# A four-layer graph network on one core: another order of the PE work of layers 2 and 3

## The chip, the cores and the metric

One core of one Trainium2 chip. The metric is the device time of one execution in microseconds (us). The kernel before took 2206.6 us (median of 4 runs, 2201.6 to 2208.3, so within 0.3%). Engines are named as in the profile: PE (matrix multiply), PEld (its weight loads), DVE, ACT, POOL, SP.

## The reference, cut to what matters

`x` is 128 graphs x 64 nodes x 256 features in fp32. Four residual layers follow each other; the change touches only the last two, which are attention inside one graph:

```python
h = relu(layernorm(x)); x = x + L2(h)     # layer 2: one head, + adj, causal mask, softmax, @ Wo
h = relu(layernorm(x)); x = x + L3(h)     # layer 3: four heads, mask adj == 0, softmax
```

Layers 0 and 1 (graph convolutions and LSTM windows) end at about 1752 us of 2206.

## The kernel before: the parts that matter

The kernel works through 16 chunks of 512 rows. Layers 2 and 3 of a chunk are four generators, each cut into units by `yield`. A table says in which order PE does the units; **only PE's order is fixed by hand**. DVE, ACT and POOL get their order from the scheduler, which works with the dependences and its own idea of durations.

```python
def rsqrt(dst, src, eps):                                     # for every layer norm, on POOL
    nc.gpsimd.tensor_scalar(dst, src, eps, None, op0=OP.add)                      # L80
    nc.gpsimd.tensor_tensor(dst, dst, mhalf[:, : dst.shape[1]], OP.pow)           # L81
...
def layernorm_relu(dst, src, name):     # names: st, mv (DVE), rstd (POOL), nmr (DVE), h (ACT)
    ...                                 # suffix _e: the norm of layer 2, _f: of layer 3
def softmax(s, n, name):                # n = 16 for layer 3, 4 for layer 2
    nc.vector.tensor_reduce(mx, s, AX.X, OP.max)                                  # L507
    nc.gpsimd.tensor_tensor(s, s, mx[...], OP.subtract)                           # L508
    nc.scalar.activation(s, s, AF.Exp)                                            # L509
    nc.vector.tensor_reduce(sm, s, AX.X, OP.add)                                  # L511
    nc.vector.reciprocal(rs, sm)                                                  # L513
    nc.vector.tensor_mul(s, s, rs[:, :, None].to_broadcast([P, n, T]))            # L514
...
# A = layer2_scores: [layer norm, transposes tc_e] [q, L558 is the copy of half of it] [v] [scores L567, softmax]
# B = layer2_out:    [transposes of the softmax] [output, added to x]
# C = layer3_scores: [layer norm, transposes tc_f] [q, k] [scores L616, softmax] [v]
# D = layer3_out:    [transposes L523, copies att: L528 on ACT, L530 on DVE] [output L643, store]
ROUND = (("A", 0), ("A", 0), ("A", 0), ("D", -2), ("C", -1), ("D", -2), ("C", -1), ("B", 0),
         ("A", 1), ("B", 0), ("C", -1), ("C", -1))
...
with tc.manual_schedule(engines={mybir.EngineType.PE}):
    unit("A", 0)
    for c in range(NCH + 2):
        for stage, d in ROUND:
            unit(stage, c + d)
```

`("C", -1)` in round c is the next unit of layer 3's scores for chunk c - 1.

Of the kernel before, what the change touches and what calls it, by code (L numbers as in the profile page):

```python
# [19 lines left out]
def kernel(  # L20
# [23 lines left out]
    B, T, D = x.shape  # L44
# [11 lines left out]
    NCH = B * T // CH  # L56
# [403 lines left out]
    with tc.tile_pool(name="w2", bufs=1) as w2p, tc.tile_pool(name="l2", bufs=2) as l2:  # L460
# [169 lines left out]
        def layer3_out(c):  # L630
# [14 lines left out]
            for r in range(2):  # L645
# [4 lines left out]



        stages = {"A": layer2_scores, "B": layer2_out, "C": layer3_scores, "D": layer3_out}
        ROUND = (("A", 0), ("A", 0), ("A", 0), ("D", -2), ("C", -1), ("D", -2), ("C", -1), ("B", 0),
                 ("A", 1), ("B", 0), ("C", -1), ("C", -1))
        units = {}

        def unit(stage, c):
            if 0 <= c < NCH:
                if (stage, c) not in units:  # L660
                    units[stage, c] = stages[stage](c)
                next(units[stage, c])

        with tc.manual_schedule(engines={mybir.EngineType.PE}):
            unit("A", 0)
            for c in range(NCH + 2):
                for stage, d in ROUND:
                    unit(stage, c + d)


# [44 lines left out]
```

## Time and profile before

| | before |
|---|---|
| median of 4 runs | 2206.6 us |
| span of the profiled run | 2205.7 us |
| PE busy | 2101.8 us (95%) |
| layers 2 and 3: one steady round | 26.20 us |
| wait of layer 2's scores for q (L567 for L558) | 1.09 to 1.15 us in each of 13 rounds |
| waits of the last two softmax transposes (L523) | 6.64 and 4.92 us |

A wait in square brackets in a timeline is the idle time of that engine just before the row and what ended it.

### The profile page before, as it was taken

How to read it: one execution, taken by the hardware profiler on the slowest of the kernel's cores; microseconds unless marked ns; L12 is line 12 of the kernel's file. 1: busy time of each engine (PE TensorE's matmuls, PEld its weight loads, DVE VectorE, ACT ScalarE, POOL GpSimd, SP SyncE). 2: the span in 40 equal slices, each digit the busy share in tenths (PEclk: the TensorE clock that was granted, in tenths of full speed). 3: DMA queues.
4: the chain of work that ended last, by engine and by line, in shares of the span. 5: the costliest groups of instructions: out<-in, count | busy, mean ns of one | idle time of the engine just before them, and what ended most of it. 6: DMA issues, size and time to landing. Idle time of an engine off the chain costs nothing.

```text
span 2205.7 us, 24595 instructions
## 1 busy us (share of the span) xinstructions
PE 2101.8 (95%) x10117; PEld 1339.7 (61%) x10117; DVE 852.5 (39%) x1848; ACT 792.1 (36%) x1433; POOL 168.8 (8%) x216
## 2 busy tenths in 40 slices
PE   6999959999999999999999999999999899999996
PEld 3553435576577468468567657656746756666664
DVE  5643433223323322332332322323222256666664
ACT  3544413233333233333333422333333344444442
POOL 2100010001000000000100100000000011112211
PEclk9999969999999999999999999999999999999998
DMA  3100050000000000000000000000000100000000
GB/s 97 58 20 0 0 186 10 10 1 10 2 9 1 10 10 1 10 10 1 10 10 1 10 10 1 0 0 1 1 0 1 34 11 21 20 21 21 21 20 29
DMA packets 30127, 37.88 MB, mean 17 GB/s; under 512 B 1856, under 2 KB 27456, under 8 KB 30016
## 3 DMA queue, kind: packets, MB, share of 16 engines
q1 hardware_dynamic: 27600, 27.89, 4.1%
q0 software_dynamic: 2256, 8.40, 1.0%
q8 instruction: 79, 1.29, 0.2%
q14 instruction: 32, 0.26, 0.0%
q10 hardware_dynamic: 160, 0.03, 0.0%
HBM read 27.93 MB, written 8.39 MB: 16 GB/s over the span
## 4 chain that ended last, share of the span: by engine, by line
PE 77%; issue 10%; DVE 7%; POOL 3%; DMA 2%; ACT 1%; SPq 0%; POOLq 0%; DVEq 0%; ACTq 0%
PE g L369 32%; PE g L376 17%; PE z L250 5%; PE z L234 3%; PE p_q L500 3%; PE u L340 3%; PE p_k L500 2%; PE v L328 2%; DMA xt<-in_x_dram 2%; PE agg_b L161 1%; PE agg_c L161 1%; PE tr L523 1%; DVE s L514 1%; PE o L643 1%; PE o L588 1%
## 5 line engine op out<-in xcount | busy, mean ns | idle before, releaser
L369 PE MATMUL g<-hT,wih 128*128 128x256 f32 (+2 forms) x2496 | 826.7, 483 | 3.6 <-DVE hT L400 2.7
L369 PEld LDWEIGHTS g<-hT,wih 128*128 128x128 f32 x2496 | 465.0, 188 | 313.1 <-issue 182.4
L382 ACT ACTIVATE gate<-g,bias 128x256 f32<-128x256 f32 (+2 forms) x624 | 350.4, 562 | 820.0 <-PE g L376 648.1
L376 PE MATMUL g<-hs,whh 128*128 128x256 f32 (+2 forms) x1536 | 435.8, 437 | 0.0
L376 PEld LDWEIGHTS g<-hs,whh 128*128 128x128 f32 x1536 | 291.3, 190 | 132.2 <-issue 62.0
L386 DVE TENSOR_TENSOR cell<-cell,gate 128x256 f32<-128x256 f32 (+2 forms) x96 | 48.7, 507 | 449.7 <-ACT gate L382 449.7
L391 DVE TENSOR_TENSOR cell<-gate,gate 128x512 f32<-128x512 f32 (+2 forms) x80 | 48.2, 602 | 213.1 <-ACT gate L382 213.1
L234 PE MATMUL z<-agg,w_sb 128*128 128x512 f32 x256 | 117.5, 613 | 8.6 <-DVE agg L227 7.2
L250 PE MATMUL z<-h,w_sb 128*128 128x512 f32 x256 | 112.1, 601 | 5.0 <-ACT h L245 5.0
L392 ACT ACTIVATE gate<-cell 128x256 f32<-128x256 f32 (+2 forms) x176 | 89.8, 510 | 50.7 <-DVE cell L391 40.3
L410 POOL COPY hn<-hT 128x512 f32<-128x512 f32 x32 | 35.9, 1197 | 784.8 <-DVE hT L400 784.8
L400 DVE TENSOR_TENSOR hT<-gate,gate 128x512 f32<-128x512 f32 (+2 forms) x80 | 48.0, 600 | 114.0 <-PE g L369 96.9
L250 PEld LDWEIGHTS z<-h,w_sb 128*128 128x128 f32 x256 | 49.4, 193 | 67.7 <-issue 57.5
L234 PEld LDWEIGHTS z<-agg,w_sb 128*128 128x128 f32 x256 | 48.6, 195 | 67.4 <-issue 49.0
L395 DVE TENSOR_TENSOR hs<-gate,gate 128x256 f32<-128x256 f32 (+2 forms) x96 | 47.7, 497 | 69.8 <-ACT gate L392 49.6
L385 DVE TENSOR_TENSOR gate<-gate,gate 128x256 f32<-128x256 f32 (+2 forms) x96 | 47.7, 497 | 55.8 <-ACT gate L382 55.8
L508 POOL TENSOR_TENSOR s<-s,mx 128x256 f32<-128x256 f32 (+1 forms) x32 | 40.3, 1259 | 340.3 <-DVE mx L507 251.8
L495 ACT COPY v<-v 128x512 f32<-128x512 f32 x64 | 37.0, 578 | 76.6 <-PE v L492 76.6
L500 PE MATMUL p_q<-hT,w_sb 128*128 128x512 f32 x128 | 61.9, 606 | 0.3 <-DVE hT L175 0.3
L500 PE MATMUL p_k<-hT,w_sb 128*128 128x512 f32 x128 | 60.1, 592 | 0.0
L492 PE MATMUL v<-w_sb,hT 128*128 128x256 f32 x256 | 59.5, 386 | 0.0
L151 ACT ACTIVATE h<-xs,nmr_b,rstd_b 128x256 f32<-128x256 f32 x64 | 34.5, 590 | 69.6 <-DVE nmr_b L149 69.6
(153 smaller groups left out, 2068.1 us busy)
## 6 DMA issues: line engine op xcount, KB each, us to landing
xt<-in_x_dram SPq DMA_DIRECT2D x32, 512.0 KB, 3.8
out_dram<-o SPq DMA_DIRECT2D x16, 512.0 KB, 2.9
wih<-in_wih_t_dram POOLq DMA_DIRECT2D x4, 1024.0 KB, 13.4
whh<-in_whh_t_dram POOLq DMA_DIRECT2D x3, 1024.0 KB, 18.2
w_sb<-in_w_dram SPq DMA_DIRECT2D x1, 768.0 KB, 4.2
wqkv_sb<-in_wqkv_dram SPq DMA_DIRECT2D x1, 768.0 KB, 4.5
w_sb<-in_w1t_dram POOLq DMA_DIRECT2D x1, 512.0 KB, 4.9
w_sb<-in_w2t_dram POOLq DMA_DIRECT2D x1, 512.0 KB, 5.8
```

What stands on the lines that cost most here:

```text
L234: nc.tensor.matmul(ps, w1_sb[:, k, m * P : (m + 1) * P], agg[:, k, :], start=(k == 0), stop=(k == KD - 1))
L250: nc.tensor.matmul(ps, w2_sb[:, k, m * P : (m + 1) * P], h1[:, k, :], start=(k == 0), stop=(k == KH - 1))
L340: nc.tensor.matmul(ps[:, i, :], v[:, k, j * P : (j + 1) * P], wg1_sb[:, k, :], start=(k == 0), stop=(k == KD - 1))
L369: nc.tensor.matmul(banks[q][:, :n].rearrange("p (j w e) -> p j w e", w=nw, e=2), wi[:, k, o], hv[:, k, :, cols, :], start=(k == 0), stop=( ...
L376: nc.tensor.matmul(banks[q][:, :n], wh[:, k, o], hs[:, k, :n], start=False, stop=(k == KD - 1))
L382: nc.scalar.activation(g[q], banks[q][:, :n], AF.Tanh if q == 2 else AF.Sigmoid, bias=bs[:, q * KD + c : q * KD + c + 1])
L386: nc.vector.tensor_mul(cell[c], cell[c], g[1])
L391: nc.vector.tensor_mul(cell[c], g[0], g[2])
L392: nc.scalar.activation(g[2], cell[c], AF.Tanh)
L400: nc.vector.tensor_mul(hv[:, c, :, cols, :], o.rearrange("p (j w e) -> p j w e", w=nw, e=2), t.rearrange("p (j w e) -> p j w e", w=nw, e=2))
L492: nc.tensor.matmul(ps[:, i, :], hT[:, k, j * P : (j + 1) * P], w[:, k, first : first + D], start=(k == 0), stop=(k == KD - 1))
L500: nc.tensor.matmul(ps, w[:, k, m * P : (m + 1) * P], hT[:, k, :], start=(k == 0), stop=(k == KD - 1))
```

## The change

Intent: q of layer 2 goes ahead of layer 3's v, so that its copies are done before the scores want them; and in the last rounds chunk 15's layer 2 and the work of its neighbours are mixed so that the last softmaxes have matmuls beside them.

```diff
-        ROUND = (("A", 0), ("A", 0), ("A", 0), ("D", -2), ("C", -1), ("D", -2), ("C", -1), ("B", 0),
-                 ("A", 1), ("B", 0), ("C", -1), ("C", -1))
+        ROUND = "A0 C-2 A0 A0 D-2 C-1 D-2 C-1 B0 A1 B0 C-1"
+        LAST = "A0 A0 A0 C-2 C-1 D-2 B0 D-2 B0 C-1 C-1 C-1 C0 C0 D-1 C0 D-1 C0 D0 D0"
...                                     # run(order, c) does the units of such a string
-            unit("A", 0)
-            for c in range(NCH + 2):
-                for stage, d in ROUND:
-                    unit(stage, c + d)
+            run("A0", 0)
+            for c in range(NCH - 1):
+                run(ROUND, c)
+            run(LAST, NCH - 1)
```

More of the change, by code (lines that the diff above doesn't have):

```diff
@@ L653, with run @@
         stages = {"A": layer2_scores, "B": layer2_out, "C": layer3_scores, "D": layer3_out}
-        ROUND = (("A", 0), ("A", 0), ("A", 0), ("D", -2), ("C", -1), ("D", -2), ("C", -1), ("B", 0),
-                 ("A", 1), ("B", 0), ("C", -1), ("C", -1))
+        ROUND = "A0 C-2 A0 A0 D-2 C-1 D-2 C-1 B0 A1 B0 C-1"
+        LAST = "A0 A0 A0 C-2 C-1 D-2 B0 D-2 B0 C-1 C-1 C-1 C0 C0 D-1 C0 D-1 C0 D0 D0"
         units = {}
-        def unit(stage, c):
-            if 0 <= c < NCH:
-                if (stage, c) not in units:
-                    units[stage, c] = stages[stage](c)
-                next(units[stage, c])
+        def run(order, c):
+            for step in order.split():
+                stage, at = step[0], c + int(step[1:])
+                if 0 <= at < NCH:
+                    if (stage, at) not in units:
+                        units[stage, at] = stages[stage](at)
+                    next(units[stage, at])
         with tc.manual_schedule(engines={mybir.EngineType.PE}):
-            unit("A", 0)
-            for c in range(NCH + 2):
-                for stage, d in ROUND:
-                    unit(stage, c + d)
+            run("A0", 0)
+            for c in range(NCH - 1):
+                run(ROUND, c)
+            run(LAST, NCH - 1)
 def kernel(**inputs):
```

## The prediction

> **What bounds the kernel now.** I read the page's busy shares, then the waits of the PE in the stretch that the change touches, then the timeline of one round engine by engine, then the timeline of the end. Times are us from the span's start.
>
> ```profile
> PE 2101.8 (95%) x10117; PEld 1339.7 (61%) x10117; DVE 852.5 (39%) x1848; ACT 792.1 (36%) x1433; POOL 168.8 (8%) x216
> ```
>
> PE is the bound: nothing else is above 39%. The change keeps every matmul and only reorders them, so it can win no more than PE idle time inside layers 2 and 3 (1755 to 2206), plus matmuls that ran at a low clock after such idle time. The PE's waits from 1720 on, columns total us, times, longest:
>
> ```profile
> PE tr L523 <- DVE s L514: 15.0, 3, 6.6
> PE s L567 <- DVE q L558: 14.8, 13, 1.2
> ```
>
> These 30 us (1.4% of the span) are nearly all there is. The second line is one wait in each of 13 rounds: layer 2's scores wait for the copy of the second half of q. The first is 3.5 us at the very start (not touched) and 6.6 and 4.9 us in the last two rounds. One steady round on PE, then on DVE, POOL and ACT (start, duration, line, work):
>
> ```profile
> 2063.83 3.60 PE L500 MATMUL p_q<-hT,wqk_sb 128*128 128x512 f32 x8
> 2072.29 1.15 PE L567 MATMUL s<-hT,q 128*64 128x64 f32 x30 [1.15 <-DVE q L558]
> 2073.37 1.09 PE L523 MATMUL tr<-ident,s 128*128 128x128 f32 x8
> 2074.30 1.04 PE L173 MATMUL tc_f<-ident,h 128*128 128x128 f32 x8
> 2075.27 1.16 PE L643 MATMUL o<-v,att 64*64 64x64 f32 x64
> ...
> 2067.65 0.16 DVE L149 SCALAR_TENSOR_TENSOR nmr_f<-mv_f,rstd_f 128x4 f32<-128x4 f32 x1 [1.96 <-POOL rstd_f L81]
> 2070.05 0.16 DVE L149 SCALAR_TENSOR_TENSOR nmr_e<-mv_e,rstd_e 128x4 f32<-128x4 f32 x1 [0.45 <-POOL rstd_e L81]
> 2070.41 1.23 DVE L514 TENSOR_TENSOR s<-s,rs 128x1024 f32<-128x1024 f32 x1
> 2071.55 0.69 DVE L558 COPY q<-p_q 128x512 f32<-128x512 f32 x1
> ...
> 2068.97 1.04 POOL L81 TENSOR_TENSOR rstd_e<-rstd_e,mhalf 128x4 f32<-128x4 f32 x1
> ...
> 2070.37 1.57 ACT L151 ACTIVATE h<-xs,nmr_e,rstd_e 128x256 f32<-128x256 f32 x3
> 2074.07 0.59 ACT L528 COPY att<-tr 128x512 f32<-128x512 f32 x1 [0.69 <-PE tr L523]
> ```
>
> The q matmuls end at 2067.26, but the copy (L558) stands last in DVE's row, behind the layer norm's nmr_e, which had to wait for POOL, and the large softmax multiply L514. PE has only the 3.55 us of layer 2's v to do meanwhile and stands still for 1.15 us. ACT is free before its copy of the attention (L528). The end of the kernel on PE:
>
> ```profile
> 2173.93 1.94 PE L523 MATMUL tr<-ident,s 128*128 128x128 f32 x8 [6.64 <-DVE s L514]
> 2196.54 1.97 PE L523 MATMUL tr<-ident,s 128*128 128x128 f32 x8 [4.92 <-DVE s L514]
> ```
>
> Both times PE has done all other work and waits for the layer 3 softmax (some 9 to 11 us of DVE, POOL and ACT after the scores), and then the eight transposes take 1.9 us, not 1.09.
>
> [...] L558 starts 4.3 us after its matmuls ended, in its place behind L514. So the order of the ACT and DVE instructions, which the scheduler makes anew for the changed kernel, counts as much as PE's order. [...] after 6.64 us idle the transposes take 1.94 us for 1.09; after the 1.15 us waits they keep to 1.09. [...]
>
> **The steady rounds.** I set t = 0 at the end of layer 3's scores, 2060.27 in the round above. Before, PE does v of layer 3 (3.56), q (3.43), v of layer 2 (3.55), layer 2's scores (1.41), attention transposes (0.93), tc_f (0.97), so the output o (L643) could start at 13.85; with the 1.15 us wait it starts at 15.00. From there to the next t = 0 are 11.20 (2075.27 to 2086.47). Round: 26.20. There are 13 such rounds.
>
> After, q goes first and v of layer 3 follows it. The q matmuls are done at 3.5, and both v's (7.1 us) cover the copies. I read the compiled instruction order of both kernels. DVE now has L558 ahead of the first nmr: at 4.96 to 5.65, in a slot that was idle. The wait of L567 (1.15) goes away, and L514 ends by about 10.95, before the transposes want it at 11.95.
>
> But the order also changed behind that. DVE's new row is: q copy, nmr_f, two mv_e, st_e, the softmax sum L511 (1.19), mv_e, st_e, reciprocal, mv_e, L514, nmr_e. The nmr_f still waits for POOL until 7.38. So the last mv_e, which was done at 8.2, comes after L511: 7.38+0.24+0.32 = 7.94 start of L511, to 9.13; mv_e and st_e to 9.53; reciprocal to 9.70; mv_e to 9.78. POOL's two steps for rstd_e take 0.16+0.31+1.04 from there: 11.29. nmr_e ends at 11.49 (before: 9.94). ACT's new row puts the four h_e activations and the two copies of layer 2's v, in the order h h v h h v, ahead of the attention copy L528. From 11.59 that is four times 0.50 plus two times 0.47, so L528 starts at 14.52 and ends at 15.08. Its transposes are ready at 12.65. The output matmuls of layer 3 need it: they start at about 15.13 and not at 13.85, a **new wait of 1.28 us at L643**. The rest of the round (attention exp, tc_f copy, q/k) I find early enough. Round after: 15.13 + 11.20 = 26.33. Thirteen rounds: 13 x 0.13 = **+1.7 us**. The wait removed comes back one step later.
>
> **The last rounds.** Before, from the last t = 0 (2138.86) to the end (2205.7) are 66.84. After, again from the end of chunk 13's scores, in the new order: q, v, scores of chunk 15 end at 8.39; v of 13 at 11.95; tc_f of 14 at 12.92; transposes of 13 and of 15 at 14.07; outputs of 13 and of 15 with about 0.2 of wait at 16.27; q/k of 14 (6.87) at 23.14; its scores, waiting some 0.6 for the last k copy as chunk 15 does today, at 25.1; v of 14 at 28.7; tc_f of 15 at 29.67. There ACT has the exp of chunk 14's softmax ahead of its half of the copy of hT, so q/k of 15 wait until 31.4 (two gaps, 1.3 together) and end at 37.85. The softmax of 14 is over by 33.6, so its transposes follow without a wait, to 38.78: the 6.64 us are gone. Scores of 15 end at 39.8, output of 14 at 40.9, v of 15 at 44.46. The softmax of 15 (mask 1.25, max 1.2, output add of 14 1.2 between, subtract 1.9, exp 1.06, sum 1.2, reciprocal and multiply 1.5, plus hand-overs) ends at 48.35: a wait of 3.9 remains. From the last transposes to the end are 9.16 today (2196.54 to 2205.7): end at 57.6. Gain 66.84 - 57.6 = **9.3 us**: about 12.6 of waits less 6.0, plus 2 to 3 us of slow matmuls after the wait that is gone.
>
> Sum: 2206.0 + 1.7 - 9.3 = **2198.4 us**; I put 2198.
>
> **Rivals.** (1) *The copy wait goes and nothing takes its place:* -14.8 in the rounds and -9.3 at the end, 2182. For it: ACT is busy only 36%, and the intent is plain. Against it: the compiled order of ACT and the dependence of nmr_e on POOL. If nmr_e came 1.3 us sooner than I find, this would be the result; I give it one in six. In between, with half the wait, 2190. (2) *The new wait is larger, or L514 comes late too:* each further 0.3 us in a round costs 3.9; with 0.5 more and only 6 us won at the end, 2208. It would need DVE instructions longer than this trace has; one in ten. (3) *The end gains little,* because the softmax of 15 still ends last: then 2203 to 2206. Against: in the new order 19 us of PE work lie between chunk 14's scores and its transposes or waits, where 3.6 do today.
>
> **Range and chances.** The three runs before span 2201.6 to 2208.3, so some 3 us are noise. Main case 2198 with 3 to 4 us either way, a tail down to rival 1: 2184 to 2205. Two per cent is 44 us, more than all the PE waits of this stretch, so faster by 2% cannot come of this; slower by 2% would need over 3 us more in every round. Same: 0.98, the others 0.01 each.
>
> **What would show each step right or wrong.** Right: no wait of L567 for L558; instead some 13 waits of L643 for the copy L528 on ACT, 1.0 to 1.5 each, rounds of 26.2 to 26.5; nmr_e about 11.4 after the scores; one transpose wait of some 4 us at the end where there were 6.6 and 4.9; waits of about 1 us for hT in the last q/k. Wrong: rounds of 25.1 with no wait at L643 (ACT's row runs earlier than I worked out), or transposes waiting for L514 in every round (DVE's row runs later).

The "low clock" is in the trace of the kernel before: 0.50 from 2171.4, inside the 6.64 us wait, to 2178.2, and from 2195.3, inside that of 4.92, to the end. Its slow matmuls after the first wait took 1.94, 1.91 and 1.48 us for 1.09, 1.04 and 1.16, together 2.0 us more. That DVE and ACT work in the compiled order was taken for granted in the sum; in one round of the changed kernel (2076.47 to 2087.46) both rows ran in the order given here.

## The result, and the profile after

The changed kernel took **2212.1 us** (median of 4, 2210.1 to 2212.6): 1.0027 of the kernel before, 95% interval 1.0009 to 1.0045. That is within 2%, but clearly slower, and outside the predicted 2184 to 2205. (Ratios here are the mean time of one kernel's fast runs over that of the other's of the same rounds, so not quite the ratio of the medians quoted.)

The two longest waits of PE from 1720 us on, in the changed kernel (total us, times, longest):

```profile
PE o L643 <- ACT att L528: 31.1, 15, 2.4
PE tr L523 <- DVE s L514: 7.5, 2, 4.1
```

The wait of L567 for q is gone, as the change intended. In its place stands the predicted wait of the output matmuls L643 for the attention copy L528 on ACT, but at 2.36 us (2.29 and 2.30 in the first two rounds), where I had worked out 1.28. It comes in 13 rounds; the other two of the 15 are of 0.29 in the last rounds. One steady round in the timelines of PE, DVE, POOL and ACT, changed kernel:

```profile
2071.52 3.70 PE L500 MATMUL p_q<-hT,wqk_sb 128*128 128x512 f32 x8
2082.06 1.20 PE L567 MATMUL s<-hT,q 128*64 128x64 f32 x32
2087.51 1.16 PE L643 MATMUL o<-v,att 64*64 64x64 f32 x64 [2.35 <-ACT att L528]
...
2081.23 1.23 DVE L514 TENSOR_TENSOR s<-s,rs 128x1024 f32<-128x1024 f32 x1
2083.70 0.16 DVE L149 SCALAR_TENSOR_TENSOR nmr_e<-mv_e,rstd_e 128x4 f32<-128x4 f32 x1 [1.24 <-POOL rstd_e L81]
...
2077.51 0.23 POOL L80 TENSOR_SCALAR rstd_f<-mv_f 128x4 f32<-128x4 f32 x1
2081.41 1.12 POOL L80 TENSOR_SCALAR rstd_e<-mv_e 128x4 f32<-128x4 f32 x1 [2.56 <-DVE mv_e L145]
2082.62 1.04 POOL L81 TENSOR_TENSOR rstd_e<-rstd_e,mhalf 128x4 f32<-128x4 f32 x1
...
2083.95 1.09 ACT L151 ACTIVATE h<-xs,nmr_e,rstd_e 128x256 f32<-128x256 f32 x2 [1.78 <-DVE nmr_e L149]
2086.88 0.58 ACT L528 COPY att<-tr 128x512 f32<-128x512 f32 x1
```

Follow it backwards. L643 waits for L528, which starts at 2086.88 although its transposes were done at 2084.28 (2083.19 + 1.09), because in ACT's row four h_e activations and two v copies stand ahead of it. h_e starts at 2083.95 because nmr_e is only there at 2083.86, because rstd_e is. And rstd_e is late by one instruction: L80, the add of epsilon to 128x4 numbers, takes **1.12 us**, while the same operation on the same shape four us earlier takes 0.23. It starts 0.18 us after the big softmax multiply L514 and ends at 2082.53, 0.07 after L514 does (2081.23 + 1.23 = 2082.46). In the groups of POOL, by form, from 1790 us on, all 13 of these adds are so (count, busy us, mean ns), first before, then after:

```profile
L80 POOL TENSOR_SCALAR rstd_e<-mv_e 128x4 f32<-128x4 f32 x13 | 3.0, 229 | 13.6 <-ACT h L151 12.5 <-DVE mv_e L145 1.0
```

```profile
L80 POOL TENSOR_SCALAR rstd_e<-mv_e 128x4 f32<-128x4 f32 x13 | 14.6, 1121 | 33.3 <-DVE mv_e L145 33.3
```

In the kernel before, this add ran beside the reduction L511, which has one input:

```profile
2068.41 1.19 DVE L511 TENSOR_REDUCE sm<-s 128x16 f32<-128x1024 f32 x1
2068.66 0.23 POOL L80 TENSOR_SCALAR rstd_e<-mv_e 128x4 f32<-128x4 f32 x1 [1.04 <-ACT h L151]
```

In the changed kernel the new DVE order puts it beside L514, whose two inputs, s and rs, both lie in SBUF.

**Where the time went, by the two traces.** The first q after the first C scores starts at about the same time (v at 1798.44 before, q at 1798.28 after). The 13 rounds that follow take 340.42 us before (1798.44 to 2138.86) and 354.83 after (1798.28 to 2153.11): +14.4. From there to the end are 66.84 before and 2210.0 - 2153.11 = 56.89 after: -9.95. With the -0.16 at the start, that is +4.3, the difference of the two spans. The +14.4 are about 13 times 0.99 (a round of 27.19 instead of 26.20) and 1.4 more in one single round of 28.60.

### The profile page after: what moved, and what is told of

It is laid out like the page before. It is cut to its first block, busy times and chain, and to the rows that moved or that the text cites. A ratio compares the mean times of both kernels' runs of the same rounds, so it can differ in the third digit from the quotient of the medians.

```text
span 2210.0 us, 24610 instructions
## 1 busy us (share of the span) xinstructions
PE 2098.0 (95%) x10117; PEld 1336.5 (60%) x10117; DVE 848.8 (38%) x1848; ACT 787.7 (36%) x1433; POOL 179.9 (8%) x216
## 4 chain that ended last, share of the span: by engine, by line
PE 78%; issue 9%; DVE 5%; ACT 3%; DMA 2%; POOL 2%; SPq 0%; POOLq 0%; DVEq 0%; ACTq 0%
PE g L369 32%; PE g L376 17%; PE z L250 5%; PE p_q L500 4%; PE z L234 3%; PE u L340 3%; PE p_k L500 2%; PE v L328 2%; PE v L492 2%; DMA xt<-in_x_dram 2%; PE agg_b L161 1%; PE agg_c L161 1%; ACT h L151 1%; PE o L643 1%; PE o L588 1%
## 5 line engine op out<-in xcount | busy, mean ns | idle before, releaser
L500 PE MATMUL p_q<-hT,wqk_sb 128*128 128x512 f32 x128 | 59.9, 611 | 0.4 <-DVE hT L175 0.4
```

The lines of the kernel that those rows point to most:

```text
L500: nc.tensor.matmul(ps, w[:, k, m * P : (m + 1) * P], hT[:, k, :], start=(k == 0), stop=(k == KD - 1))
```

## The experiments

My theory after the result: (a) the end of the kernel gained as predicted; (b) the rounds lost because h_e stands ahead of the attention copy on ACT; (c) the size of the loss was wrong because the add on POOL is shut out while a multiply with two SBUF inputs runs on DVE (1.12 us for 0.23). Rivals: the two parts are not independent; the attention copy is late for another reason; the add is slow for a reason of POOL's own, such as 2.56 us of idleness before it. The last has already one trace line against it: in the changed kernel's end an add came after 7.95 us of idleness and took 0.23:

```profile
2172.81 0.23 POOL L80 TENSOR_SCALAR rstd_f<-mv_f 128x4 f32<-128x4 f32 x1 [7.95 <-DVE mv_f L145]
```

All results below were correct. Times are medians; runs of one call share their runs of the kernel before (2206.3 us for the first four, 2206.1 for the last two).

### 1. Only the new end

```diff
-        ROUND = "A0 C-2 A0 A0 D-2 C-1 D-2 C-1 B0 A1 B0 C-1"
-        LAST = "A0 A0 A0 C-2 C-1 D-2 B0 D-2 ...
+        ROUND = "A0 A0 A0 D-2 C-1 D-2 C-1 B0 A1 B0 C-1 C-1"      # as before
+        LAST = "A0 A0 A0 C-1 D-2 B0 D-2 ...
```

> The kernel before with its own order in the rounds, and only the new order in the last rounds. From the two traces: the last 66.84 us of the kernel before became 56.9 in the changed kernel. My theory (the end gained about 10 us, the rounds lost about 14): 2206.6 - 10 = 2196.6, between 2195 and 2199, no wait of L643 in the rounds, 13 waits of L567 of 1.15. Rival (the gain at the end depends on the new rounds, for example on v of layer 3 coming later): less than 5 us gained.

Measured: 2198.5 us (ratio 0.9966, 0.9951 to 0.9980). 13 waits of L567 as before, none of L643 in the rounds. The gain is 7.8 us rather than 10: with v of chunk 13 already done, chunk 15's softmax transposes have less work ahead of them and wait 2.13 us. So the new end is worth 8 us here and nearly 10 together with the new rounds.

### 2. Only the new rounds

```diff
-            for c in range(NCH - 1):
+            for c in range(NCH + 2):
                 run(ROUND, c)
-            run(LAST, NCH - 1)
```

> The new order of q and v in the rounds alone; the last rounds follow the old order. My theory: 13 rounds of 27.2 to 27.3 instead of 26.2, so about 14 us slower than before: 2219 to 2223. If the two parts do not simply add, the sum of this difference and that of the run with the new end alone misses the measured +4.5 us of the full change by more than 3 us.

Measured: 2221.1 us (ratio 1.0061, 1.0044 to 1.0078), rounds of 27.20 and again one of 28.59. The loss of 14.7 and the gain of 7.8 add to +6.9, the full change gave +5.5: they add up to within 1.4 us, which is less than the wait of 2.13 that only run 1 has, and not more than the scatter of the runs. The new q order, which was to save 1.15 us a round, is what makes the kernel slower.

### 3. The attention copy ahead of h_e on ACT

```diff
 def transposed(...):
-                    nc.scalar.copy(d, ps[:, : w * P])
+                    ins = nc.scalar.copy(d, ps[:, : w * P])
+                    if n > NJ:
+                        att_copy["last"] = ins
 def layer2_scores(c):
-            layernorm_relu(h, xt, f"e{c}")
+            if att_copy:
+                with tc.issue_after(att_copy["last"].ins):   # order of issue on that engine only
+                    layernorm_relu(h, xt, f"e{c}")
+            else:
+                layernorm_relu(h, xt, f"e{c}")
```

> The changed kernel with one constraint on ACT's order: the layer norm activations of the next chunk's layer 2 (h_e) may be issued only behind the attention copy L528 of layer 3; nothing else is changed. Theory (the new wait of L643 comes from h_e standing ahead of L528 in ACT's row): the wait goes, rounds of 24.8 (13.57 + 11.2) instead of 27.2, total about 2212 - 31 = 2179 to 2184. Rival (L528 is late for another reason, such as its transposes or layer 2's v copies): rounds stay above 26.5, total above 2204. A third possibility: h_e now comes too late for its transposes (tc_e), which would show as waits of tc_e for ACT.

Measured: **2177.5 us** (2175.7 to 2180.3), 0.9871 of the kernel before (0.9856 to 0.9885), a little below the 2179 to 2184 expected. The waits of PE from 1720 us on begin:

```profile
PE tr L523 <- DVE s L514: 7.6, 2, 4.1
PE wt L476 <- DMA wo_sb<-in_wo_dram: 4.9, 1, 4.9
PE at_d L187 <- POOL hn L410: 2.6, 1, 2.6
```

In the rounds PE waits for nothing any more. A round, on PE and ACT:

```profile
2057.82 1.16 PE L651 MATMUL o<-v,att 64*64 64x64 f32 x64
...
2056.61 0.59 ACT L528 COPY att<-tr 128x512 f32<-128x512 f32 x1 [0.74 <-PE tr L523]
2057.10 0.60 ACT L151 ACTIVATE h<-xs,nmr_e,rstd_e 128x256 f32<-128x256 f32 x1
```

(L651 is L643 with the added lines.) The order of instructions on PE, DVE and POOL is that of the changed kernel; only ACT's differs. The copy is issued as soon as its transposes are done, h_e behind it still comes in time for the next chunk, and rounds are 24.77 us. The order of ACT's instructions was the cause of the whole new wait. The v copies of layer 2 still stand ahead of the copy and do no harm. The add on POOL still takes 1.12 us here (13 of 13), now without consequence.

### 4. The softmax multiply in two halves

```diff
-            nc.vector.tensor_mul(s, s, rs[:, :, None].to_broadcast([P, n, T]))
+            for i in range(0, n, min(n, 8)):
+                g = slice(i, i + min(n, 8))
+                nc.vector.tensor_mul(s[:, g, :], s[:, g, :], rs[:, g, None].to_broadcast([P, min(n, 8), T]))
```

> The changed kernel with the softmax multiply L514 of layer 3 cut into two instructions of half the width. Theory (the eps add L80 for rstd_e on POOL takes 1.12 us and not 0.23 because it is shut out while the two-input multiply on DVE runs): L80 gets in after the first half and takes about 0.5 to 0.6, the wait at L643 falls by about 0.5, total about 2205; or, if DVE keeps POOL out over both halves, L80 stays at about 1.1 to 1.2 and the total at 2212. Rival (POOL is slow here for its own reasons, such as a start after 2.6 us of idleness): L80 stays at 1.12 whatever DVE does, and its end no longer falls together with the end of a multiply.

Measured: 2210.8 us, against the kernel before 1.0020 (1.0005 to 1.0035). The total lies between the two forms of my expectation and says little; the groups of POOL say more:

```profile
L80 POOL TENSOR_SCALAR rstd_e<-mv_e 128x4 f32<-128x4 f32 x13 | 7.7, 589 | 33.3 <-DVE mv_e L145 33.3
L81 POOL TENSOR_TENSOR rstd_e<-rstd_e,mhalf 128x4 f32<-128x4 f32 x13 | 17.3, 1332 | 1.1
```

The add gets in after the first half (0.59 us instead of 1.12), and then, beside the second half, the power L81 grows from 1.04 to 1.33. The add of 0.5 to 0.6 us is as expected; that the power would then be slowed was not, so the wait at L643 fell by 0.2 us and not by 0.5. POOL's slowness follows DVE's multiply and not POOL's idleness, which is 2.56 us in both cases. Both steps together gained only 0.24 us (1.92 instead of 2.16), so rounds fell from 27.19 to 26.99; two of the 13 rounds were long ones of 28.5, one more than in the changed kernel, which took back some 1.5 us of the 2.6 won in 13 rounds.

### 5. One operand of the multiply in PSUM

```diff
-            rs = small.tile([P, n], F32, tag=f"rs{n}", name=f"rs_{name}")
+            if rs is None:
+                rs = small.tile([P, n], F32, tag=f"rs{n}", name=f"rs_{name}")
 def layer3_scores(c):
-            softmax(s, NJ * HEADS, f"3_{c}")
+            softmax(s, NJ * HEADS, f"3_{c}", rs=banks[1][:, : NJ * HEADS])   # a bank of the scores, read by then
```

This is the cleanest test: the order of the instructions on PE, DVE and ACT is that of the changed kernel to the last one; only the address of 16 numbers per partition differs.

> The changed kernel with one operand moved: the reciprocal that the layer 3 softmax multiply reads lies in a PSUM bank that is free by then, so that multiply has one SBUF input and not two. The order of the instructions on PE, DVE and ACT is the same as in the changed kernel, to the last instruction. Theory (a multiply with two SBUF inputs shuts the eps add of rstd_e on POOL out): that add takes 0.23 again in all 13 rounds, the wait at L643 falls from 2.36 to about 1.5, rounds of 26.3 to 26.4 as I had predicted, total about 2200 (2198 to 2203). Rival (the add is slow for another reason, or the multiply still holds it off): 1.12, rounds of 27.2, 2212.

Measured: **2198.7 us** (median of 5, 2197.7 to 2200.2), ratio 0.9966 (0.9952 to 0.9980). The multiply (L515; the profile gives the PSUM operand the name of its bank, s) and the add, first in one round, then all 13 adds:

```profile
2070.24 1.22 DVE L515 TENSOR_TENSOR s<-s,s 128x1024 f32<-128x1024 f32 x1
2070.42 0.23 POOL L80 TENSOR_SCALAR rstd_e<-mv_e 128x4 f32<-128x4 f32 x1 [2.56 <-DVE mv_e L145]
L80 POOL TENSOR_SCALAR rstd_e<-mv_e 128x4 f32<-128x4 f32 x13 | 3.0, 228 | 33.3 <-DVE mv_e L145 33.3
```

and the wait at the output matmuls in a round (L644 is L643):

```profile
2075.62 1.16 PE L644 MATMUL o<-v,att 64*64 64x64 f32 x64 [1.47 <-ACT att L529]
```

The add still starts 0.18 us into the multiply and after the same 2.56 us of idleness, and takes 0.23 again; rounds are 26.31 us (predicted for the changed kernel: 26.33), and the total is what I had predicted for the changed kernel, 2198. The long rounds of 28.6 are gone as well.

### 6. Both remedies

The edits of 3 and 5 together.

> The operand of the multiply in PSUM and, besides, the attention copy ahead of h_e on ACT. Theory (the shut-out costs time only because h_e stands ahead of the attention copy): no further gain, 2176 to 2180 as with the order alone, although the eps add takes 0.23 again. Rival (the shut-out also costs elsewhere): clearly below 2175.

Measured: 2179.2 us (2177.1 to 2182.9), ratio 0.9878 (0.9865 to 0.9891), rounds of 24.77 as with 3 alone. The add takes 0.23, and it gains nothing (2177.5 in run 3, where it takes 1.12): in these two runs no wait of PE in the rounds hangs on it. The version to keep is 3.

## Why the prediction was wrong, by its own steps

- **The wait for q goes** (-1.15 in each of 13 rounds): right. L567 waits no more.
- **A new wait comes at L643, for the attention copy behind h_e on ACT**: right in place, cause and number of rounds; run 3 shows the cause by taking it away.
- **Its size, 1.28 us, and the round of 26.33**: wrong; 2.36 and 27.19. The term that was mis-sized is in the sentence "POOL's two steps for rstd_e take 0.16+0.31+1.04 from there: 11.29". I took 0.31 from the start of the add to the start of the power, out of the kernel before, where the add takes 0.23. In the changed kernel the add takes 1.12 and that step 1.21 (2081.41 to 2082.62), so the chain nmr_e, h_e, L528, L643 came 0.86 late: nmr_e ended 12.34 after the scores and not 11.49, L643 began at 15.99 and not 15.13. (The other 0.22 of the wait are no time: PE arrived sooner than I had it, as layer 2's scores take 1.13 when they are not interrupted, and not 1.41.) The rounds lost 14.4 us where I had 1.7. Of these 12.7 the 0.86 make 11.2 in 13 rounds; the rest is the long round, which I had not foreseen. Run 5 takes away nothing but the collision, and the time is 2198.7.
- I had moved L514 and the chain of rstd_e to the same moment in my own sum, and treated two engines as independent. The runs show that here they were not: the add takes 0.23 beside a one-input reduction (before), 1.12 beside the two-input multiply with its end 0.07 after the multiply's (after), 0.59 with half a multiply (run 4), 0.23 with one operand in PSUM (run 5). The mechanism behind it no trace shows. Nor did the trace of the kernel before show the collision: all its adds of L80 take 0.22 to 0.24.
- **The end gains 9.3**: right, 9.95. The gap of 6.64 is gone; the predicted 3.9 us before the last transposes were 4.08; the two gaps for hT in the last q/k were 0.60 together where I had 1.3. A little of the 9.95 is when the clock happened to fall (see below): the last eight transposes took 1.07 and not 1.97. In runs 3, 5 and 6, where they took 1.82 to 1.94, the same end takes 57.2 to 57.5, a gain of 9.4 to 9.7.
- **Rivals.** Number 1 (nothing takes the place of the wait) was wrong for this kernel, and its figure of 2182 is about what run 3 reaches by asking for it. Number 2 ("the new wait is larger", one in ten) is what happened, though not for the reason that it named: no DVE instruction was longer, one on POOL was. It was put too low: a chain of durations taken from another order of instructions needs only one that does not hold, and the error multiplies by 13. A range up to 2213 was called for. Number 3 (the end gains little) did not come; its "19 us of PE work" is the stretch from chunk 14's scores to the last wait (25.1 to 44.46), while to chunk 14's own transposes the prediction's line has 12.75 and the trace 12.43.
- **Same within 2%**: right. A slip without effect: "nothing else is above 39%" passes over PEld at 61%, in the line shown; with PE at 95% the two are busy together for at least 56% of the span.

**The round of 28.60 us.** In it, right after the 2.36 us wait, the 64 output matmuls took 1.99 us in place of 1.16, and the next q was slow as well. The clock records of the trace settle what it was:

```profile
1922.94 1.99 PE L643 MATMUL o<-v,att 64*64 64x64 f32 x64 [2.36 <-ACT att L528]
...
1891.90:1895.32 3.42, 1.48 (x14) 1.24 (x12) 2.11 (x5) 3.14 (x7) 0.61 (x1) 1.00 0.00 0
1919.21:1922.62 3.41, 1.37 (x13) 1.13 (x11) 2.03 (x5) 3.23 (x7) 0.61 (x1) 1.00 0.00 0
1922.62:1926.04 3.42, 3.10 (x66) 2.46 (x67) 2.08 (x5) 1.06 (x3) 0.00 (x0) 0.50 0.00 0
1926.04:1929.45 3.41, 3.41 (x10) 1.50 (x9) 0.51 (x2) 0.58 (x1) 0.00 (x0) 1.00 0.46 154
```

(A line of the table of stretches: start and end, length, busy time of PE, PEld, DVE, ACT and POOL with the number of instructions, then the granted clock.) The clock was 0.50 for one stretch of 3.41 us and 1.00 on both sides. In the traces of the kernels before and after all changes of the clock stand a whole number of 3.41 us apart (13 and 15 intervals, from 3.41 to 1419.94 = 416 x 3.4133), so I cut the time into these windows, in runs 2 and 4 as well. PE stood still for 2.04 us of the window before the fall; one round earlier, for 1.94 us of its window, and no fall came (second and first line of the table; the ends of matmuls are modelled, so the busy times are not exact). The 13 rounds of run 2 show nearly the same figures, 1.93 without a fall and 2.04 with one; in run 4 the two windows with 2.12 and 2.15 were followed by falls, and none of its others in the rounds, up to 1.87. Eight windows are 27.31 us and a round is 27.2, so the gap moves some 0.1 us further into one window with each round, until 2 us of it lie there; then the long round sets it back (0.76 us in the round after). In run 5, with waits of 1.40 to 1.48, no round was long. The limit is that of these rounds and no rule: near the end of run 4 a fall followed a window with 1.87 us idle.

## What to carry to other kernels

Changing the order on the bounding engine can change the scheduler's order on the others, as it did here on DVE and ACT; read the new order of each engine, and where a chain hangs on it, fix it by hand: one issue constraint on ACT turned +0.3% into -1.3%. When work is moved in time, ask for each instruction on POOL what DVE will be doing beside it, as a duration measured in the old order need not hold in the new one (the add here: 0.23 us, then 1.12). And remove waits one at a time with the next one worked out: here the copy that had been hidden behind one wait was the next.

## What else the traces show

- A short POOL instruction against back-to-back DVE instructions: with the multiply cut in two, POOL got in between the halves (add of 0.23 at 0.59) and its next instruction, beside the second half, took longer (1.04 at 1.33). The remedy that worked here, one of the two inputs in PSUM, brought the add from 1.12 back to 0.23; the multiply itself took 1.23 and 1.22 us.
- How idle a window of 3.41 us was before the clock fell: in the steady rounds 2.04 us were followed by a fall and 1.94 were not. So gaps of only 2.15 to 2.37 us slowed some rounds (1 of 13 in the changed kernel and in run 2, 2 of 13 in run 4), and where a gap lay decided which matmuls paid: after the gap of 4.08 us the changed kernel's last transposes still took 1.07 us for eight, since the clock fell from 1.00 to 0.50 at 2202.52, just behind them, and the output matmuls took 1.98; in run 3, after 4.09, the transposes were slow already (1.94).
- The power operation on POOL (L81) took 1.04 us for 128x4 elements wherever I read POOL's rows (before, after, runs 3, 5 and 6; 1.33 for rstd_e in run 4, beside the second half of the multiply), against 0.23 for the add; in the setup of the kernel before 0.74 for 128x2 and 0.58 for 128x1.
